# A transformer kernel on one Trainium2 core: later projections, earlier norms, idle products, signs on GpSimd and half of the stacks on ScalarE

## The chip, the core and the metric

The kernel runs on one core of a Trainium2 chip. A core has TensorE (PE in the profile; PEld is its loading of weights), VectorE (DVE), ScalarE (ACT), GpSimd (POOL) and SyncE (SP), which run side by side, each with its own queue of instructions in a fixed order; semaphores make one wait for another. SBUF is the core's working memory, PSUM the memory that TensorE writes its products to. The metric is the time of one execution on the device in microseconds (us), as a median over runs. Everything is computed in float32.

## The reference

Input x has 8 batches of 512 tokens of 256 elements. Four sublayers follow one another, each added to the residual:

```python
x = x + attn_a(layernorm(x))   # 8 heads of 64, keys and values through a rank of 64, softmax
x = x + ffn(layernorm(x))      # two layers, below
x = x + attn_b(layernorm(x))   # 16 heads of 16, below
x = x + ffn(layernorm(x))      # the same weights again

# ffn, each of two layers:
q, k, v = split(shift_token(x) @ wqkv)               # 8 heads of 64
q, k = rotary_xpos(l2norm(q) * qs, l2norm(k) * ksc)
x = x + local_attention(q, k, v) @ wo                # windows of 128, looking back one window
h = layernorm(shift_token(x)) @ w1 + b1              # to 2 x 682
a, g = split(h);  x = x + (a * gelu(g)) @ w2 + b2

# attn_b:
scores = dot * dot / (|q|^2 + |k|^2 - 2 * dot + 1e-6)   # causal
out = softmax(scores) @ v @ w_out + b_out
```

## The kernel before

The 8 batches are worked off in two groups of 4. A group passes through ten stages: attention_a, block x (attention_f and feedforward of layer 0, then of layer 1), attention_b, and block y (the same four as block x). All residuals of a group lie in SBUF; a batch is four tiles of 128 tokens (NT = 4). So the kernel has 8 attention_f stages, 8 feedforward stages and 2 attention_b stages.

A stage is a head and a `run`. While a stage runs, it calls `ahead()`, which emits a piece of the next stage's head; what is left of the head is emitted after it. Within a stage the order of each engine's instructions is written by hand: under `order_keeper` every instruction is tied to the one before it on its engine in program order.

**attention_f** (L453) works on nt = 16 tiles of 128 queries. `a_step` (L732) handles tile `step`: two units (even and odd, four heads each) of scores, maxima (L614), exponentials, `divided` (L679: the reciprocal of the sums on DVE, then four ACT operations that scale the probabilities), `turn` (L646, transposes on PE into PSUM), `keep_turned` (L657, the copy to SBUF on DVE) and `values` (L671). `keep_values` (L690) copies the tile's output, `project` (L696) multiplies it with wo, `add` (L706) adds it to `ys`, the stage's residual. Each step projects the tile of the step before. In the last steps (`projecting` false) no queries and keys of further tiles are left to be made.

**feedforward** (L805) goes through the four batches: `hidden` makes the products with w1 and gelu, `output` (L879) those with w2. `batch(n)` (L907) slips the statistics, norms and transposes of the next batches (`others`) in between.

**attention_b** (L960) works on units: one of 4 query tiles of a batch, a pair of heads (`qp`) and one to four column blocks `js`. There are 22 units a batch, 88 a group. Ahead of them stand, per batch, `normalized` (L963: `row_statistics` L256, whose inverse root is on POOL at L252 and L253, and `normalize_rows` L266) and `stacks_and_values` (L977): transposes, then 8 `side_piece`s and 2 `value_piece`s. A side piece makes one stack of heads of queries (left) or keys (right): products on PE (L1000), their squares on ACT (L1010), the squared norms added by PE (L1013), and `keep_side` (L1022 to L1028), which writes the stack st_b to SBUF with a bias and a scale, on DVE. The pieces of batch 0 are the stage's head; those of the next batches are laid one by one into the steps of the batch before (`a_piece`, L1261), and two more pieces (L1232, a turn prt and a projection pp) follow each query tile.

One unit passes through five steps: products den and dot (L1099, PE); the inverse of den by Ln and Exp (L1112, L1113, both through `function`, L227, on ACT); its error t and refinement r (L1118, L1122, DVE); squares of dot (L1128, ACT) with the causal mask (L1131, POOL); `highest` (L1134): on DVE a fused product with maximum per head (L1139) and the negation of the maxima (L1149); the exponentials (L1157 through L227, ACT), biased with the negated maxima; transposes ppt (L1169, PE), the copy pt (L1174, DVE) and the values o (L1184, PE). `each_part` (L1270) writes the order of one step by hand: the products of unit s, the dot of s-1, the maxima of s-2, the turns of s-3 and, every other step, the values of two units. The norms of batches 1, 2 and 3 are issued in steps 0 and 1, 20 and 21, 42 and 43 of the group.

In PSUM the pool `ps_s` has three buffers of two banks, for den, dot and the pieces; `ps_mm` and `ps_o` have one each, for ppt and o.

Of the kernel before, what the change touches and what calls it, by code (L numbers as in the profile page):

```python
# [11 lines left out]
F32 = mybir.dt.float32  # L12
# [5 lines left out]
P = 128  # L18
# [11 lines left out]
W1_COLS = 2 * FULL + GATES + REST  # L30
DEPTH = 2
LN_EPS = 1e-5
EPS_B = 1e-6
# [4 lines left out]
GELU_TABLES = "gelu_and_others"  # L38
Piece = namedtuple("Piece", "heavy first act second dve", defaults=(None, None, None, None))
Unit = namedtuple("Unit", "n product inverse error refine squares highest exponentials turn keep_turned values project")  # L40
ISSUE_ORDER = mybir.DependencyInfo(mybir.DependencyClass.NoSync, mybir.DependencyReason.DATA)
# [4 lines left out]
def kernel(  # L46
# [101 lines left out]
    vec_b = load(b_vec, [P, 2, 4, 2], "vec_b")  # L148
    sel_b = load(b_sel, [P, 2, P], "sel_b")

    def weights_f(l, name):
# [132 lines left out]
    def halves_of(rows):  # L284
        return [rows[:, :, 0:P], rows[:, :, P:D]]


# [165 lines left out]
    def attention_f(batches, l, g, ys, first_layer):  # L453
# [225 lines left out]
        def divided(unit):  # L679

            at, quad = divmod(unit, 2)
            p, s = ps[unit], sums[at]
            some = slice(4 * quad, 4 * quad + 4)
            nc.vector.reciprocal(s[:, some], s[:, some])
            for odd in range(2):
                for j in range(2):
                    h = 4 * quad + 2 * j + odd
                    nc.scalar.activation(p[:, odd, j], p[:, odd, j], AF.Identity, scale=s[:, h : h + 1])
# [20 lines left out]

        nt, nu = len(tiles), 2 * len(tiles)  # L710

        def on(f, at, count=nt):
# [10 lines left out]
        def rows(at):  # L723
            b, t = tiles[at]
            if first_layer and t == 0:
                normalize_rows([xs[b]], [ys[b]], *stats.pop(b))

# [4 lines left out]
        def a_step(step):  # L732

            even, odd = 2 * step, 2 * step + 1
            projecting = step + 2 < nt
            if not projecting:
                on(turn, even - 1, nu)
                on(keep_turned, even - 1, nu)
# [10 lines left out]
            if not projecting:  # L749
# [3 lines left out]
                on(maxima, odd, nu)  # L753
            on(divided, even, nu)
            on(rotate, step + 2)
            if projecting:
# [6 lines left out]
            if projecting:  # L763
                on(exponentials, odd, nu)
                on(keep_values, step - 1)
                on(turn, even, nu)
                on(keep_turned, even, nu)
                on(norms, step + 2)
                on(turn_tile, step + 1)
                on(keep_tile, step + 1)  # L770
                on(project, step - 1)
            else:
                on(project, step - 1)
                on(turn_tile, step + 1)
                on(keep_tile, step + 1)
                on(exponentials, odd, nu)
                on(turn, even, nu)
                on(keep_turned, even, nu)
            on(divided, odd, nu)
            on(values, even, nu)  # L780
            on(add, step - 1)
            on(statistics, step + 5)
# [21 lines left out]

    def feedforward(batches, l, g, ys, last, finish):  # L805
        w1, w2 = weights_g(l, g)
# [100 lines left out]
        def batch(n):  # L907

            others = [(statistics, n + 1), (rows, n + 1), (shift, n + 2)]
            others += [(lambda b, k=k: columns(b, k), n + 1) for k in range(2)]  # L910
            for _ in hidden(batches[n]):
                if others:
                    part, m = others.pop(0)
                    if m < len(batches):
                        with kept_order():
                            part(batches[m])
                yield
# [16 lines left out]
        def run(ahead):  # L934
            for n, b in enumerate(batches):
                if n:
                    for _ in batch(n):
                        if n == len(batches) - 1:
                            ahead()
                            ahead()  # L940
                output(b, made.pop(b))

        return head(), run

    def feedforward_block(batches, g, finish):

        ys = {}

        def attention(l):
            if l == 0:  # L950
                for b in batches:
                    ys[b] = resid.tile([P, NT, D], F32, tag=f"y{b % GROUP}", name=f"y_{g}_{b}")
            return attention_f(batches, l, f"{g}{l}", ys, l == 0)

        for l in range(DEPTH):
            yield lambda l=l: attention(l)
            yield lambda l=l: feedforward(batches, l, f"{g}{l}", ys, l == DEPTH - 1, finish)


    def attention_b(batches, g):  # L960
        wl_b, wr_b, wv_b, wo_b, bv_b = weights_b(g)

        def normalized(b):  # L963

            got = {}

            def statistics():
                got["mv"], got["rstd"] = row_statistics([xs[b]], f"b{b}")

            def rows():  # L970
                yr = pool.tile([P, NT, D], F32, tag="yr", name=f"yr_b{b}", bufs=1)
                normalize_rows([xs[b]], [yr], got["mv"], got["rstd"])
                state[b] = {"yr": yr}

            return [Piece(False, dve=statistics), Piece(False, dve=rows)]

        def stacks_and_values(b):  # L977
# [16 lines left out]
            def side_piece(side, w, j):  # L994
# [27 lines left out]
                def keep_side():  # L1022
# [5 lines left out]
                    )  # L1028

                return Piece(True, project, squared, norms, keep_side)  # L1030

# [33 lines left out]
        def prologue(b):  # L1065
            for piece in normalized(b):
                whole(piece)
                yield
            for piece in stacks_and_values(b):
                whole(piece)  # L1070
                yield
# [5 lines left out]

        state = {}

        def unit(b, i, qp, js, first, last):  # L1080
# [45 lines left out]
            def squares(dot):  # L1126
                num = pool.tile([P, 2, T], F32, tag="p", name=f"num_{n}", bufs=3)
                nc.scalar.activation(num[:, :, :cols], dot[:, :, :cols], AF.Square, scale=-0.5)  # L1128
                for m in range(len(js)):
                    own = per_head(num)[:, :, m, past:]  # L1130
                    nc.gpsimd.tensor_add(own, own, causal.unsqueeze(1).to_broadcast([P, 2, P]))  # L1131
                return num

            def highest(num, r):  # L1134
# [3 lines left out]
                for at, (a, m, h) in enumerate(heads):  # L1138
# [9 lines left out]
                    )  # L1148
                nc.vector.tensor_scalar_mul(most[:, 8 : 8 + nh], most[:, :nh], -1.0)  # L1149
                return most  # L1150
# [48 lines left out]
            def project(sums):  # L1199
# [9 lines left out]
                def turned():  # L1209
                    got["prt"] = ps_s.tile([P, 2, 4, P], F32, tag="s", name=f"prt_{n}")[:, 0]  # L1210
                    for k in range(4):
                        nc.tensor.transpose(got["prt"][:, k, :], rows[:, k * P : (k + 1) * P], ident)

# [19 lines left out]

            return Unit(n, product, inverse, error, refine, squares, highest, exponentials, turn, keep_turned, values, project)

# [7 lines left out]

        def run(ahead):

# [15 lines left out]
            def a_piece(s):  # L1261
# [3 lines left out]
                for some, may in ((projections, s % 2 or len(projections) % 2 == 0), (prologues, ready), (projections, True)):  # L1265
                    if some and may:
                        return some.popleft()
                return Piece(False)

            def each_part(s):  # L1270
# [6 lines left out]
                if with_values:  # L1277
                    for u in (s - 5, s - 4):
                        projections.extend(units[u].project(sums.pop(u)))
                piece = a_piece(s)  # L1280

# [26 lines left out]
                if unit_of(2):  # L1308
                    most[s - 2] = units[s - 2].highest(num[s - 2], r.pop(s - 2))
                if unit_of(3):  # L1310
                    units[s - 3].keep_turned(turned, pt[s - 3], 0)
                    turned = units[s - 3].turn(num.pop(s - 3), 1)
# [5 lines left out]
                if unit_of(3):  # L1318
                    units[s - 3].keep_turned(turned, pt[s - 3], 1)
                do(piece.dve)  # L1320
                if norms:
                    do(norms.popleft().dve)

            for step in range(count + 5):
                if step % each == 0:
# [4 lines left out]
                    if following < len(batches):  # L1330
                        if following == 1:
                            norms.extend(normalized(batches[1]))
                        prologues = deque(stacks_and_values(batches[following]))
                elif step % each == each - 2 and step // each + 2 < len(batches):
                    norms.extend(normalized(batches[step // each + 2]))
                with kept_order():
                    each_part(step)
                if step > count - 6:
                    ahead()
            with kept_order():  # L1340
                while projections:
                    whole(projections.popleft())

        return prologue(batches[0]), run

# [6 lines left out]
    for g in range(NB // GROUP):  # L1352
        batches = list(range(g * GROUP, (g + 1) * GROUP))
        stages.append(lambda batches=batches, g=g: attention_a(batches, g))
        stages.extend(feedforward_block(batches, f"{g}x", None))
        stages.append(lambda batches=batches, g=g: attention_b(batches, g))
        stages.extend(feedforward_block(batches, f"{g}y", store))
# [106 lines left out]
```

## Time and profile before

| what | value |
|---|---|
| median of 3 runs | 4530.55 us (4523.1 to 4535.95) |
| the profiled execution's own time | 4521.22 us |
| its span | 4519.4 us |
| mean granted TensorE clock | 0.965 of full speed |
| PE busy | 4197.8 us (93%) |
| DVE busy | 3138.2 us (69%) |
| ACT busy | 2695.9 us (60%) |
| POOL busy | 1183.9 us (26%) |
| attention_b, first step of a group to its drain | 1038 to 1532 us, 3288 to 3776 us |

The profile records each instruction with its engine, its line and its tiles. A group of instructions is written "line engine operation out<-in", with the number of instructions, their busy time and the mean of one, and the idle time of the engine ahead of them with what ended it. In the slices each digit is a tenth of busy time in a fortieth of the span; PEclk is the clock granted to TensorE. Names end in what they belong to: `_b` is attention_b, `_f0x` attention_f of layer 0 in block x, `_g0x` its feedforward.

### The profile page before, as it was taken

How to read it: one execution, taken by the hardware profiler on the slowest of the kernel's cores; microseconds unless marked ns; L12 is line 12 of the kernel's file. 1: busy time of each engine (PE TensorE's matmuls, PEld its weight loads, DVE VectorE, ACT ScalarE, POOL GpSimd, SP SyncE). 2: the span in 40 equal slices, each digit the busy share in tenths (PEclk: the TensorE clock that was granted, in tenths of full speed). 3: DMA queues.
4: the chain of work that ended last, by engine and by line, in shares of the span. 5: the costliest groups of instructions: out<-in, count | busy, mean ns of one | idle time of the engine just before them, and what ended most of it. 6: DMA issues, size and time to landing. Idle time of an engine off the chain costs nothing. (4 is left out here: it accounts for less than half of the span.)

```text
span 4519.4 us, 68348 instructions
## 1 busy us (share of the span) xinstructions
PE 4197.8 (93%) x25504; PEld 2569.5 (57%) x25504; DVE 3138.2 (69%) x7688; ACT 2695.9 (60%) x6316; POOL 1183.9 (26%) x1076
## 2 busy tenths in 40 slices
PE   9999999998888799999999999999988878999999
PEld 5666656554544465566556665565544544655655
DVE  6678647738999787377466786476389997864773
ACT  5767527617788676177167674275178786752761
POOL 0024224312222243143100242242122222422431
PEclk9999999999898799999999999999998888999999
DMA  2000000000000000000100000000000000000000
GB/s 81 1 22 4 23 22 3 22 5 20 1 1 1 19 3 6 4 23 13 52 29 1 20 3 23 22 3 24 3 20 1 1 1 20 3 6 22 3 4 23
DMA packets 51083, 63.22 MB, mean 14 GB/s; under 512 B 6336, under 2 KB 45504, under 8 KB 50752
## 3 DMA queue, kind: packets, MB, share of 16 engines
q1 hardware_dynamic: 50752, 58.85, 3.9%
q8 instruction: 203, 3.33, 0.3%
q14 instruction: 128, 1.05, 0.1%
HBM read 46.28 MB, written 4.19 MB: 11 GB/s over the span
## 5 line engine op out<-in xcount | busy, mean ns | idle before, releaser
L1169 PE MATMUL ppt_b<-ident,num_b 128*128 128x128 f32 x1280 | 245.9, 315 | 152.8 <-DVE pt_b L1174 136.0
L1131 POOL TENSOR_TENSOR num_b<-num_b,causal 128x256 f32<-128x256 f32 x256 | 197.1, 783 | 663.5 <-ACT num_b L1128 572.8
L1169 PEld LDWEIGHTS ppt_b<-ident,num_b 128*128 128x128 f32 x1280 | 153.3, 156 | 339.5 <-ACT num_b L227 99.9
L227 ACT ACTIVATE num_b<-num_b,most_b 128x512 f32<-128x512 f32 (+3 forms) x512 | 280.6, 554 | 23.8 <-DVE most_b L1149 20.0
L1139 DVE CUSTOM_DVE_ANT_0 num_b<-num_b,r_b 128x512 f32<-128x512 f32 (+3 forms) x512 | 249.9, 535 | 5.9 <-POOL num_b L1131 5.9
L1174 DVE COPY pt_b<-ppt_b 128x512 f32<-128x512 f32 (+1 forms) x352 | 223.6, 635 | 36.3 <-PE ppt_b L1169 34.9
L227 ACT ACTIVATE r_b<-den_b 128x1024 f32<-128x1024 f32 (+1 forms) x176 | 166.3, 945 | 136.1 <-PE den_b L1099 70.3
L1099 PE MATMUL den_b<-st_b,st_b 18*128 18x384 f32 (+3 forms) x1024 | 239.8, 523 | 7.3 <-DVE t_b L1118 5.1
L227 ACT ACTIVATE p_a<-s_a,nm_a 128x512 f32<-128x512 f32 x256 | 173.7, 684 | 109.7 <-DVE nm_a L376 105.4
L1099 PE MATMUL dot_b<-st_b,st_b 16*128 16x384 f32 (+3 forms) x1024 | 215.1, 522 | 1.4 <-ACT num_b L1128 1.4
L376 DVE TENSOR_REDUCE nm_a<-s_a 128x2 f32<-128x1024 f32 x128 | 156.5, 1223 | 69.6 <-PE s_a L372 69.6
L1118 DVE TENSOR_TENSOR t_b<-den_b,r_b 128x1024 f32<-128x1024 f32 (+1 forms) x176 | 196.8, 1118 | 9.8 <-ACT r_b L227 8.9
L227 ACT ACTIVATE p_f0y<-p_f0y,nm_f0y,rn_f0y 128x256 f32<-128x256 f32 (+1 forms) x256 | 143.8, 564 | 91.4 <-DVE nm_f0y L614 91.3
L227 ACT ACTIVATE p_f1y<-p_f1y,nm_f1y,rn_f1y 128x256 f32<-128x256 f32 (+1 forms) x256 | 143.8, 564 | 91.1 <-DVE nm_f1y L614 91.0
L1122 DVE SCALAR_TENSOR_TENSOR r_b<-t_b,r_b 128x1024 f32<-128x1024 f32 (+1 forms) x176 | 197.8, 1124 | 0.1
L227 ACT ACTIVATE p_f0x<-p_f0x,nm_f0x,rn_f0x 128x256 f32<-128x256 f32 (+1 forms) x256 | 143.7, 564 | 84.9 <-DVE nm_f0x L614 84.8
L227 ACT ACTIVATE p_f1x<-p_f1x,nm_f1x,rn_f1x 128x256 f32<-128x256 f32 (+1 forms) x256 | 143.7, 564 | 83.8 <-DVE nm_f1x L614 80.1
L390 ACT ACTIVATE p_a<-p_a,sums_a 128x512 f32<-128x512 f32 x256 | 171.8, 720 | 27.0 <-DVE sums_a L388 27.0
L227 ACT ACTIVATE r_b<-r_b 128x1024 f32<-128x1024 f32 (+1 forms) x176 | 172.5, 980 | 5.6
L517 POOL TENSOR_TENSOR ro_f1x<-ro_f1x,rs_f1x 128x512 f32<-128x512 f32 x64 | 80.3, 1277 | 361.1 <-DVE nm_f1x L614 144.1
L517 POOL TENSOR_TENSOR ro_f0x<-ro_f0x,rs_f0x 128x512 f32<-128x512 f32 x64 | 80.3, 1276 | 361.3 <-DVE nm_f0x L614 144.1
L1128 ACT ACTIVATE num_b<-dot_b 128x1024 f32<-128x1024 f32 (+1 forms) x176 | 164.8, 937 | 0.0
(345 smaller groups left out, 11249.3 us busy)
## 6 DMA issues: line engine op xcount, KB each, us to landing
x<-in_x SPq DMA_DIRECT2D x8, 512.0 KB
out<-x SPq DMA_DIRECT2D x8, 512.0 KB
wf_0x<-in_f_wqkv SPq DMA_DIRECT2D x2, 1536.0 KB
wf_0y<-in_f_wqkv SPq DMA_DIRECT2D x2, 1536.0 KB
wf_1x<-in_f_wqkv SPq DMA_DIRECT2D x2, 1536.0 KB
wf_1y<-in_f_wqkv SPq DMA_DIRECT2D x2, 1536.0 KB
wg_0x<-in_f_w SPq DMA_DIRECT2D x2, 1386.0 KB
wg_0y<-in_f_w SPq DMA_DIRECT2D x2, 1386.0 KB
```

Source lines behind the costliest of these rows:

```text
L227: i = nc.scalar.activation(out, in_, func, **more).ins
L376: nc.vector.tensor_reduce(nm, s, AX.X, ALU.max, negate=True)
L390: nc.scalar.activation(p[:, odd], p[:, odd], AF.Identity, scale=some[:, odd : odd + 1])
L517: i = nc.gpsimd.tensor_add(ro[:, c], ro[:, c], rs[:, c]).ins
L1099: return nc.tensor.matmul(s[:, a, m * width : (m + 1) * width], lhsT=left[at, j, past:width], rhs=right[at, j, :width], start=True, stop=True,
L1118: nc.vector.tensor_mul(t[:, :, :cols], den[:, :, :cols], r[:, :, :cols])
L1122: nc.vector.scalar_tensor_tensor(r[:, :, :cols], t[:, :, :cols], 2.0, r[:, :, :cols], ALU.subtract, ALU.mult)
L1128: nc.scalar.activation(num[:, :, :cols], dot[:, :, :cols], AF.Square, scale=-0.5)
L1131: nc.gpsimd.tensor_add(own, own, causal.unsqueeze(1).to_broadcast([P, 2, P]))
L1139: nc.vector.tensor_tensor_reduce(out=s4[:, a, m, :], in0=s4[:, a, m, :], in1=r4[:, a, m, :], scale=-1.0, scalar=LOWEST, op0=ALU.mult, op1= ...
L1169: nc.tensor.transpose(ppt[:, k, :], p[:, a, k * P : (k + 1) * P], ident)
L1174: nc.vector.tensor_copy(pt[:, a, :nblocks, :], ppt[:, :nblocks, :])
```

## The change

It consists of six edits.

1. attention_f: projections pass through a queue (`due`). Steps nt-4 and nt-3 no longer project; the steps after them project twice, once behind `divided(even)` and once behind `keep_turned(even)`. The last unit's division is two DVE products in place of four ACT operations.
2. The norms of batches 0, 1 and 2 of attention_b are made in the last feedforward of block x, those of batch 3 at step 6. The rows lie in the space of `y{b}`.
3. Steps 0 and 1 of attention_b (`EARLY_STEPS`) become part of its head; in that feedforward they are emitted ahead of the last `output`.
4. `kept_awake` is a product of 128x128x512 whose result nothing reads. One stands behind each turn prt (16 a group) and one in each step without a piece (26 a group).
5. The masks on POOL are issued after `highest`, and the negation of the maxima moves from DVE to POOL, ahead of them.
6. Of the 64 stacks those with odd j are written by ACT (`keep_side_late`, the last ACT operation of the step), the others by DVE as before.

```diff
+    scaled_b = const.tile([P, 2, 4], F32, name="scaled_b")
+    nc.vector.tensor_mul(scaled_b, vec_b[:, :, :, 0], vec_b[:, :, :, 1])
...
             nc.vector.reciprocal(s[:, some], s[:, some])
+            if unit == nu - 1:
...
+                for odd in range(2):
+                    nc.vector.tensor_mul(
...
+                return
...
+            on(due.append, step - 1)
+            deferring = step in (nt - 4, nt - 3)
...
             on(divided, even, nu)
+            if not projecting:
+                project_next()
+                add_projected()
...
-                on(project, step - 1)
+                if not deferring:
+                    project_next()
             else:
-                on(project, step - 1)
...
                 on(keep_turned, even, nu)
+                project_next()
...
-            on(add, step - 1)
+            add_projected()
...
+            if norms and n == 2:
+                others.append((lambda b: [part(batches[0]) for part in norms], n))
+            if norms and n == 3:
+                others = [(lambda _, m=m, part=part: part(batches[m]), n) for m in (1, 2) for part in norms]
...
+                if norms and n == len(batches) - 1:
+                    for _ in range(EARLY_STEPS):
+                        ahead()
                 output(b, made.pop(b))
...
+                def keep_side_late():
...
+                    nc.scalar.activation(
+                        state[b][name][:, j, :],
+                        got.pop("pu"),
+                        AF.Identity,
+                        bias=scaled_b[:, side, j : j + 1],
+                        scale=vec[:, 1:2],
+                    )
+
+                if j % 2:
+                    return Piece(True, project, squared, norms, None, keep_side_late)
...
+        def kept_awake(space):
+
+            nc.tensor.matmul(
+                space[:, 1].rearrange("p k c -> p (k c)"), lhsT=ident, rhs=wl_b[:, 0, :], start=True, stop=True
+            )
...
-                nc.vector.tensor_scalar_mul(most[:, 8 : 8 + nh], most[:, :nh], -1.0)
+                nc.gpsimd.tensor_scalar(most[:, 8 : 8 + nh], most[:, :nh], -1.0, 0.0, ALU.mult, ALU.add)
...
+                    kept_awake(prt)
...
-                return Piece(False)
+                return Piece(False, first=lambda: kept_awake(ps_s.tile([P, 2, 4, P], F32, tag="s", name=f"idle_b{s}")))
...
+                if unit_of(1):
+                    units[s - 1].masked(num[s - 1])
...
                 do(piece.dve)
+                do(piece.late)
...
-                elif step % each == each - 2 and step // each + 2 < len(batches):
-                    norms.extend(normalized(batches[step // each + 2]))
+                elif step == 6:
+                    norms.extend(Piece(False, dve=lambda part=part: part(batches[-1])) for part in norms_b)
...
+        def head():
+            yield from prologue(batches[0])
+            for _ in range(EARLY_STEPS):
+                next(rest)
+                yield
```

## The prediction

> **What bounds the kernel now.** I read the page's busy times and its 40 slices first, then windows by stage, then DVE's timeline of one step and the waits there. In every table the columns are PE, PEld, DVE, ACT, POOL (busy us, instructions); the windows add PEclk, DMA share and GB/s.
>
> ```profile
> PE 4197.8 (93%) x25504; PEld 2569.5 (57%) x25504; DVE 3138.2 (69%) x7688; ACT 2695.9 (60%) x6316; POOL 1183.9 (26%) x1076
> ...
> PE   9999999998888799999999999999988878999999
> ...
> DVE  6678647738999787377466786476389997864773
> ...
> PEclk9999999999898799999999999999998888999999
> ```
>
> PE is the bound nearly everywhere. In two places, slices 10 to 14 and 30 to 34, its share and clock sink while DVE's rises: attention_b. From the first step of each group to the drain:
>
> ```profile
> 1038.00:1532.00 494.00, 406.25 (x3248) 239.24 (x3246) 463.47 (x1074) 402.65 (x805) 128.88 (x158) 0.87 0.01 5
> 3288.00:3776.00 488.00, 402.10 (x3184) 235.38 (x3184) 462.96 (x1072) 399.90 (x803) 127.01 (x156) 0.88 0.01 3
> 500.00:550.00 50.00, 43.32 (x257) 27.42 (x256) 27.66 (x84) 24.70 (x63) 7.18 (x7) 0.97 0.13 41
> ```
>
> In attention_b DVE works 463.5 of 494 us (94%) and 463.0 of 488: it is the bound, and its 25 to 30 us of idle time are the only other thing to win. ACT (82%) and PE (82%, partly at half clock) stand close behind. The third line is the tail of an attention_f: PE loses 6.7 of 50 us. The kernel has eight such tails.
>
> Four windows of 3.4 us show what half clock follows:
>
> ```profile
> 1135.40:1138.80 3.40, 2.41 (x14) 1.02 (x12) 3.37 (x9) 2.38 (x6) 0.83 (x2) 0.97 0.00 0
> 1138.80:1142.20 3.40, 3.40 (x14) 2.92 (x12) 3.37 (x9) 3.26 (x4) 0.13 (x1) 0.53 0.00 0
> 1248.00:1251.40 3.40, 2.00 (x34) 1.33 (x37) 3.37 (x8) 3.37 (x5) 0.31 (x1) 1.00 0.00 0
> 1251.40:1254.80 3.40, 2.97 (x15) 0.96 (x7) 3.37 (x9) 3.21 (x7) 0.43 (x1) 1.00 0.00 0
> ```
>
> With only scores and turns in it (14 instructions, 2.41 us busy) the first was followed by one at 0.53. The third held 34 instructions, values among them, was busy less (2.00 us), and the clock stayed. A step with more products of any kind keeps its clock.
>
> **The change part by part.** The maxima's signs, one step of DVE:
>
> ```profile
> 1119.60 0.08 DVE L1139 DVE_READ_ACCUMULATOR2_ANT most_b<- 128x1 f32 x1
> 1119.72 0.17 DVE L1149 TENSOR_SCALAR most_b<-most_b 128x2 f32<-128x2 f32 x1
> 1119.80 0.55 DVE L1174 COPY pt_b<-ppt_b 128x384 f32<-128x384 f32 x1
> ```
>
> The copy starts 0.08 after the negation and the negation 0.04 after the accumulator's end, so each holds DVE between 0.08 and 0.20 us. I take 0.15: 88 units a group give 13.2 us (7 to 18). On POOL the same work is short only when free:
>
> ```profile
> L252 POOL TENSOR_SCALAR rstd_f0y<-mv_f0y x2: 194/194/194, 1286.9 to 1335.1; 128x4 f32<-128x4 f32 x2
> L252 POOL TENSOR_SCALAR rstd_b<-mv_b x3: 1072/1072/1675, 1043.7 to 1283.0; 128x4 f32<-128x4 f32 x3
> ```
>
> An operation of 4 elements took 194 ns, or 1072 to 1675 ns where DVE read two SBUF tiles (the 1675 began 0.18 us after the 1.20 us r_b<-t_b,r_b of L1122). The negation starts behind the second maximum, and what DVE runs then is the copy out of PSUM, one PSUM tile (0.55 us). So I take about 0.3 us. Behind it in POOL's queue stand the masks of the next unit; they wait for the squares anyway (the mask at 1121.04, over a microsecond after). Who waits for the sign is the exponential: in four steps it began 0.32, 0.90, 1.36 and 1.89 us after the negation's end. ACT's own work (squares, 1.01 us) covers it; I price it at nothing, and at up to 1.5 us a step if that cover is gone (below).
>
> The Trainium skill, GPSIMD Engine Reference, section 1 (Specifications), says that GpSimd shares its SBUF interfaces with VectorE and contends with DVE instructions that have two SBUF inputs. The 194 against 1675 ns agree; it speaks against this move, and is the mechanism of the rival that ends slower.
>
> The stacks: 32 a group, of which 24 are made inside the steps; half of these, 12, go to ACT as its last operation of the step.
>
> ```profile
> L1026 DVE TENSOR_SCALAR st_b<-pu_b,vec_b 128x512 f32<-128x512 f32 x24 | 19.4, 810 | 5.4 <-PE pu_b L1013 5.3
> L1010 ACT ACTIVATE sq_b<-pu_b,vec_b x64: 669/687/692, 990.4 to 3641.7; 128x512 f32<-128x512 f32 x64
> ```
>
> DVE loses 12 x 0.81 = 9.7 us; ACT gains 12 x 0.69 = 8.3 (same shape, same source), 403 to 411 of some 463. It lies in ACT's wait for the next den (0.4 to 1.2 us behind such a step), so I price it at nothing; without that cover it is the 8.3.
>
> The norms: of four batches a group, three move into the last feedforward of block x, the fourth to step 6. Inside the steps batches 1 to 3 were made, so DVE loses two, each about 1.6 (statistics) + 1.3 us (rows): 5.8. In the feedforward DVE has idle time (20.25 busy of 50 us in 600 to 650, PE 49.84), so they cost nothing there. Their POOL step held DVE and starved PE: steps with norms took 9.93, 8.70 and 9.95 us against 5.2 to 5.5; that excess, some 12 us a group, is mostly half clock and idle DVE, and I count it below.
>
> The idle products: 16 with the turns and 26 in steps with no piece, two instructions each. A pair of the same shape (128x128x512) with its norm takes 1.88 us for four instructions, so 0.94 each, 39 us a group of PE's time (406 to 445 of some 463). PE waits for DVE's pt copy 1.3 to 1.5 us in a step (136 us over 176 steps in the group of ppt_b, 0.77 on average), which covers it. What they buy is clock. DVE idles 30.5 and 25.0 us a group: I take 6 back, since starts, drains and the last piece's wait stay; bounds -5 (products late before den) and +18. The three edits before free DVE 13.2 + 9.7 + 5.8 = 28.7 us; as ACT and PE would then be as full as DVE is, I let three quarters through, 21.5 (bounds 0 and 28.7).
>
> The Trainium skill, TensorE: Matmul & The Clock Gate, section HAM oscillation, wants no PE gap over about 3.4 us. By that rule alone the idle products would be needless and the sum loses their 12 us. The trace differs: the window at 1135.4 held no gap over 1 us and still lost its clock.
>
> Two early steps: attention_b's start leaves PE idle 3.3 us (1039 to 1043) and then at half clock; the scores of steps 0 and 1 now stand before the last output's 96 products (L884, 0.38 us each, 36 us of PE), under which ACT and DVE can work them off. I take 4 us a group, that idle time and a little of the half clock (0 to 8; the Exp table load, 1.28 us, moves with them).
>
> The attention_f tails: in 505 to 545 PE waits
>
> ```profile
> PE o_f0x L671 <- DVE pt_f0x L657: 2.8, 3, 1.3
> PE ppt_f0x L646 <- ACT p_f0x L688: 2.0, 2, 1.3
> PE pp_f0x L701 <- DVE oT_f0x L693: 0.6, 1, 0.6
> ```
>
> Two projections of four products (L701, 0.379 us each, 1.5 a projection) now lie in those waits for pt, and work that stood elsewhere goes: 0.8. The last division is
>
> ```profile
> 526.94 1.28 ACT L221 ACT_TABLE_LOAD   x1
> 528.23 1.71 ACT L688 ACTIVATE p_f0x<-p_f0x,sums_f0x 128x256 f32<-128x256 f32 x4
> ```
>
> over 1.7 us on ACT behind a table load, against two DVE products of 128x512 (a like product at L548 takes 0.684): ready perhaps 1 us sooner, as DVE is not full there. Together 1.5 us a tail (0 to 3.5), eight times: 12.
>
> **Sum.** A group: 21.5 + 6 + 4 = 31.5; two: 63; with the tails 75. The profiled execution took 4521.22 us (span 4519.4), so 4446 for it. The runs' median of 4530.55 stands 9.3 above, so **4455** for the median.
>
> **Rivals.** (A) The sum: 4455, and 4430 to 4490 as its own range.
> (B) All of it converts: DVE stays the only bound, the clock holds. 2 x (28.7 + 18 + 8) + 8 x 3 = 133: 4397. For it: DVE at 1.00 in nearly every full-clock slice. Against: ACT at 411 + waits.
> (C) Three engines are full: what DVE loses becomes waits for den and for exponentials, and the idle products take PE's slack. Only starts and tails remain, 4 + 6: about 4520. For it: in group 0 ACT waits 33.4 us for dot, 38 times, so PE sets steps too:
>
> ```profile
> ACT r_b L227 <- PE dot_b L1099: 33.4, 38, 2.8
> ACT num_b L227 <- DVE most_b L1149: 5.5, 4, 3.0
> ```
>
> (D) Slower. The sign on POOL falls into a two-input DVE operation in most steps. At 1.68 against 0.17 it is 1.5 us late; less the four slacks above that is 1.18, 0.60, 0.14 and 0: mean 0.48, x 176 = 84 us; with the stacks' 24 x 0.69 = 17 no longer covered, against 12 + 8 from tails and starts: +81, the extreme. At 1.07 (0.9 late) only one slack in four is overrun, 0.58/4 x 176 = 26: about +22. Middle +50: 4580. It decides once the negation takes over about 1 us in half of the steps. For it: ACT waits only 4 times (5.5 us) for the maxima now, in the second of these lines, because DVE brings the signs itself. Against: the copy behind.
> (E) The idle products don't hold the clock but cost: 84 x 0.94 = 79 us of PE, a third uncovered, 26, and no 12: 4455 + 38 = 4493.
>
> **How the numbers follow.** A 0.46, B 0.16, E 0.08, C 0.11, D 0.19. A run differs from no change when it is more than 0.3% off (4517 to 4544). Faster: A, B, E and a fifth of C: 0.73; within: the rest of C, 0.08; slower: D, 0.19. The range reaches from B's 4395 up over C to 4545 and leaves out most of D and B's far side.
>
> **What would show it.** DVE's busy time in the 88 steps falls from 463 to about 435 a group, the stretch itself to about 465; PEclk rises from 0.87 to over 0.93, and the group of the exponentials still waits little for most_b. POOL's negation at about 0.3 us shows the move right, at over 1 us in many steps rival D. PE's wait for pt_b shrinks by the idle products if they are covered; ACT's wait for dot grows in C. The tails' PE idle falls from 6.7 to about 5. I am wrong if DVE's work falls and the step doesn't shorten.

## The result, and the profile after

| | before | after |
|---|---|---|
| median of 4 runs | 4528.1 us (4523.1 to 4535.95) | 4463.74 us (4459.31 to 4469.85) |
| span of the profiled execution | 4519.4 us | 4457.5 us |

The ratio is 0.9857, with a 95% interval of 0.9838 to 0.9876: 64 us faster, where 75 were forecast. The page of the changed kernel:

```profile
PE 4198.1 (94%) x25672; PEld 2537.4 (57%) x25672; DVE 3112.7 (70%) x7497; ACT 2697.5 (61%) x6316; POOL 1209.4 (27%) x1252
...
DVE  6678637747999787377466786477389997864773
...
PEclk9999999999999999999999999999999999999999
```

The clock's dip in slices 10 to 14 and 30 to 34 is gone. To compare like with like I cut both attention_b stages from the third step (the first that lies in the stage in both kernels) to the last. Windows of the kernel before, then of the changed one (columns as in the prediction):

```profile
1045.30:1531.90 486.60, 402.46 (x3193) 236.33 (x3192) 458.62 (x1064) 397.59 (x800) 127.30 (x157) 0.87 0.00 1
3293.10:3777.80 484.70, 399.93 (x3192) 233.90 (x3192) 460.00 (x1064) 397.49 (x799) 127.30 (x156) 0.88 0.00 1
```

```profile
1036.80:1501.20 464.40, 401.70 (x3235) 223.69 (x3234) 431.68 (x932) 402.34 (x811) 135.83 (x236) 0.96 0.02 6
3252.30:3720.10 467.80, 406.28 (x3234) 225.87 (x3234) 431.22 (x932) 402.66 (x811) 135.83 (x235) 0.95 0.02 6
500.00:550.00 50.00, 47.47 (x274) 29.30 (x271) 30.63 (x88) 23.36 (x60) 7.53 (x7) 1.00 0.13 42
```

DVE works 26.9 and 28.8 us less; the stretch is only 22.2 and 16.9 us shorter, so DVE's idle time in it grew, from 28.0 and 24.7 us to 32.7 and 36.6. The attention_f tail loses 2.5 of 50 us of PE where it lost 6.7.

From the last output product of the feedforward to that third step, before and after:

```profile
1034.90:1045.30 10.40, 6.89 (x82) 5.50 (x80) 6.19 (x14) 4.96 (x5) 3.12 (x4) 0.89 0.61 209
```

```profile
1035.30:1036.80 1.50, 1.50 (x27) 1.05 (x26) 1.40 (x4) 0.00 (x0) 0.81 (x2) 1.00 0.06 7
```

10.4 us became 1.5, in both groups; the feedforward, which now also makes norms and two steps, takes 2.7 and 4.4 us longer. Stage by stage, the difference of the two spans (61.9 us) comes from the steps (22.2 + 16.9 = 39.1), the starts (6.2 + 4.5 = 10.7) and the attention_f and feedforward stages outside (12.0 together, those behind attention_b's drain 0.7 us slower each).

The signs on POOL (least, median and longest in ns), and the last division of an attention_f on DVE's timeline. In names such as `f0x` the digit is the group (0 or 1), not the layer as said above; both layers of a block share the name. This is the first attention_f of group 0:

```profile
L1205 POOL TENSOR_SCALAR most_b<-most_b x176: 191/192/202, 1035.6 to 3743.0; 128x2 f32<-128x2 f32 x128, 128x4 f32<-128x4 f32 x32, 128x8 f32<-128x8 f32 x16
```

```profile
526.36 0.18 DVE L690 RECIPROCAL sums_f0x<-sums_f0x 128x4 f32<-128x4 f32 x1 [0.61 <-ACT p_f0x L230]
526.57 1.29 DVE L697 TENSOR_TENSOR p_f0x<-p_f0x,sums_f0x 128x512 f32<-128x512 f32 x2
```

None of the 176 negations was held up: 162 of them ran beside VectorE's copy pt_b. In the steps ScalarE waited 3.7 us a group for a sign, 5 and 6 times. The division ends 1.5 us after its reciprocal begins; before it was 3.0 (526.95 to 529.94), behind the table load.

### The profile page after: what moved, and what is told of

The parts are those of the page before. It is cut to its first block, busy times and chain, and to the rows that moved or that the text cites. A ratio compares the mean times of both kernels' runs of the same rounds, so it can differ in the third digit from the quotient of the medians.

```text
span 4457.5 us, 68762 instructions
## 1 busy us (share of the span) xinstructions
PE 4198.1 (94%) x25672; PEld 2537.4 (57%) x25672; DVE 3112.7 (70%) x7497; ACT 2697.5 (61%) x6316; POOL 1209.4 (27%) x1252
## 4 chain that ended last, share of the span: by engine, by line
PE 75%; DVE 13%; ACT 8%; POOL 2%; issue 1%; DMA 0%; SPq 0%; POOLq 0%; ACTq 0%; DVEq 0%
PE pu_g1x L891 3%; PE pu_g0x L891 3%; PE pu_g0y L891 3%; PE pu_g1y L891 3%; PE s_a L378 3%; PE o_a L414 3%; PE ppt_a L403 3%; PE pqk_f0y L481 2%; PE pqk_f1y L481 2%; PE pqk_f1x L481 2%; PE pqk_f0x L481 2%; DVE pt_b L1230 2%; DVE r_b L1176 2%; PE ppt_b L1225 2%; DVE num_b L1195 2%; PE pp_a L432 1%
## 5 line engine op out<-in xcount | busy, mean ns | idle before, releaser
L1225 PE MATMUL ppt_b<-ident,num_b 128*128 128x128 f32 x1280 | 226.5, 294 | 104.8 <-DVE pt_b L1230 84.2
L1225 PEld LDWEIGHTS ppt_b<-ident,num_b 128*128 128x128 f32 x1280 | 139.3, 144 | 289.7 <-ACT num_b L230 92.4
L1153 PE MATMUL den_b<-st_b,st_b 18*128 18x384 f32 (+3 forms) x1024 | 212.2, 476 | 4.8 <-ACT yT_b L1031 4.1
L1153 PE MATMUL dot_b<-st_b,st_b 16*128 16x384 f32 (+3 forms) x1024 | 195.7, 477 | 0.0
```

The lines of the kernel that those rows point to most:

```text
L1153: return nc.tensor.matmul(s[:, a, m * width : (m + 1) * width], lhsT=left[at, j, past:width], rhs=right[at, j, :width], start=True, stop=True,
L1225: nc.tensor.transpose(ppt[:, k, :], p[:, a, k * P : (k + 1) * P], ident)
```

## The experiments

Each kernel was run beside the kernel before; the ratio is to that one, and the changed kernel's own is 0.9857. "Span" is the profiled execution's, beside 4457.5 (changed) and 4519.4 (before). W is the theory that DVE's work set the steps, C that the clock did.

| run | median us | ratio (95% interval) | span us |
|---|---|---|---|
| e1_no_idle | 4474.88 | 0.9894 (0.9879 to 0.9909) | 4467.5 |
| e2_sign_dve | 4477.73 | 0.9904 (0.9889 to 0.9919) | 4473.3 |
| e3_stacks_dve | 4462.25 | 0.9871 (0.9855 to 0.9888) | 4460.2 |
| e4_idle_first | 4444.11 | 0.9826 (0.9809 to 0.9842) | 4446.4 |
| e5_only_idle | 4516.46 | 0.9976 (0.9967 to 0.9986) | 4515.0 |
| e6_no_early | 4490.68 | 0.9923 (0.9908 to 0.9938) | 4489.2 |
| e7_tail_act | 4475.84 | 0.9887 (0.9871 to 0.9902) | 4469.4 |
| e8_tail_only | 4511.25 | 0.9963 (0.9948 to 0.9978) | 4509.7 |
| e9_first_dve | 4439.84 | 0.9809 (0.9794 to 0.9823) | 4437.9 |
| e10_norms_back | 4485.77 | 0.9909 (0.9892 to 0.9925) | 4483.1 |
| e11_three_early | 4451.95 | 0.9838 (0.9823 to 0.9852) | 4449.6 |

How far one profile can be trusted: e3 and e5 reached the first attention_f 4 us later than the kernel that each edits, in an attention_a that neither touches. A term below some 5 us can't be read from one span. The profiled execution of the changed kernel was also the fastest of its four, that of e4 the slowest of its four, so the ratios are read beside the spans.

**Clock or work.** The changed kernel without idle products, and the kernel before with them alone:

```diff
-                return Piece(False, first=lambda: kept_awake(ps_s.tile([P, 2, 4, P], F32, tag="s", name=f"idle_b{s}")))
+                return Piece(False)
...
-                    kept_awake(prt)
```

> The changed kernel (4463.7 us) without its 84 idle products. Theory W (the work taken from VectorE shortened the steps; clock matters little): half-clock time in the 88 steps goes back to some 100 us a group, but the time rises by only 4 to 14 us, to 4468 to 4478; the stretch from the third to the last step of a group (464.4 and 467.8 us) grows by 2 to 7 us. Theory C (the clock did it): the time rises by 30 to 40 us, to 4494 to 4504.

> The kernel before (4528.1 us) with the idle products alone. Theory W: the clock is held (half clock under 50 us a group against 127 and 115), VectorE's work is unchanged, and the time falls by 0 to 12 us, to 4516 to 4528; it may even rise if the products delay den. Theory C: it falls by 30 to 40 us, to 4488 to 4498.

The steps of e1 in the same cut:

```profile
1038.00:1506.60 468.60, 397.47 (x3192) 231.84 (x3191) 434.10 (x933) 403.29 (x812) 138.74 (x236) 0.89 0.02 6
3259.60:3728.60 469.00, 396.99 (x3192) 228.74 (x3192) 433.11 (x933) 403.33 (x812) 138.79 (x235) 0.90 0.02 6
```

The clock falls back to 0.89 and 0.90, half-clock time to 99 and 96 us a group as W expected, and the stretch grows by only 4.2 and 1.2 us. Behind the last step the half clock held for another 23.9 us in each group (3.4 in the changed kernel), 20.5 of them in one piece, and from the last step to the end of that attention_f 1.3 and 1.5 us are lost. In all +10 us, as W had it, of which 1.7 lie in the two attention_a stages, which the edit doesn't touch; the ratio's rise of 0.0037 (17 us, with intervals that just don't overlap) is higher. Put into the kernel before, the same products take 8.5 and 2.1 us off the steps and save 4.4 us of span and 0.0024 of ratio (11 us), with half clock at 51 and 75 us a group, a little above what W expected. C is out: the clock is worth about a sixth of the result by the spans, a quarter by the ratios, and a third of what the trace places lies behind the steps.

**The signs** back on VectorE:

```diff
-                nc.gpsimd.tensor_scalar(most[:, 8 : 8 + nh], most[:, :nh], -1.0, 0.0, ALU.mult, ALU.add)
+                nc.vector.tensor_scalar_mul(most[:, 8 : 8 + nh], most[:, :nh], -1.0)
```

> The changed kernel with the maxima's signs back on VectorE, all else as changed. Theory W: 176 negations of about 0.15 us on VectorE, seven tenths of them felt: +15 to +26 us, 4479 to 4490; VectorE's busy time in a group's steps rises by 12 to 15 us. Theory C, or that ScalarE is now the bound: within 5 us of 4463.7.

DVE's busy time in the cut rose by 12.9 us in each group (to 444.6 and 444.1) and the span by 15.8, of it 11.2 and 2.9 in the steps. That is W's mechanism, but some 55% of the work is felt in place of seven tenths, and unevenly: in the second group most of it went into DVE's idle time (36.6 us, now 26.6). The masks stay behind `highest` in this run; what their new place is worth was not tested alone.

**The stacks** all on VectorE:

```diff
-                if j % 2:
-                    return Piece(True, project, squared, norms, None, keep_side_late)
```

> The changed kernel with all stacks written by VectorE again. Theory W: 24 stacks of 0.81 us inside the steps, seven tenths of them felt: +10 to +19 us, 4474 to 4483. Rival (ScalarE is as full as VectorE, so that moving the stacks only moved the wait): within 5 us of 4463.7, ScalarE's busy time in the steps falling by 8 us a group with no effect.

Not slower: W failed here. 12 stacks of 0.81 us came back to DVE in each group, yet its busy time rose by only 4.1 and 5.0 us, in part since its refinement r_b got shorter (by 3.6 and 2.3 us in these steps); and its idle time fell, by 2.0 and 8.9 us. The group of r_b on the pages of the changed kernel and of e3:

```profile
L1176 DVE SCALAR_TENSOR_TENSOR r_b<-t_b,r_b 128x1024 f32<-128x1024 f32 (+1 forms) x176 | 206.2, 1172 | 0.2
```

```profile
L1174 DVE SCALAR_TENSOR_TENSOR r_b<-t_b,r_b 128x1024 f32<-128x1024 f32 (+1 forms) x176 | 200.3, 1138 | 0.2
```

Before it took 1124 ns. In the changed kernel those of 128x1024 took 1.35 us on average where a POOL operation ran beside them (55) and 1.21 where none did (57).

**The idle product's place.** In the changed kernel ScalarE waits for an idle product: L1130 is `kept_awake`. ScalarE's waits in the steps (us in total, times, longest):

```profile
ACT r_b L230 <- PE den_b L1153: 16.9, 14, 6.6
ACT r_b L230 <- PE dot_b L1153: 15.4, 18, 1.9
ACT rt_b L1274 <- PE prt_b L1130: 13.6, 14, 2.3
```

```diff
+                    kept_awake(prt)
                     for k in range(4):
                         nc.tensor.transpose(prt[:, 0, k, :], rows[:, k * P : (k + 1) * P], ident)
-                    kept_awake(prt)
```

> The changed kernel with the idle product of the turn prt issued ahead of its four transposes instead of behind them. Theory F: ScalarE's copy rt waits for the idle product, since this is the last write to the tile that it reads half of (rt waits 13.6 and 17.4 us a group, 14 times each); ahead of the transposes the product falls into TensorE's wait for rb (11.5 and 11.2 us a group). The wait of rt falls below 5 us a group and the time by 6 to 20 us, to 4444 to 4458. Rival: the copy is not on the way, the wait goes and the time stays within 5 us of 4463.7.

The same line of ScalarE's waits in e4:

```profile
ACT rt_b L1274 <- PE prt_b L1269: 3.2, 7, 1.4
```

The span fell by 11.1 us, the ratio by 0.0031 (14 us), with intervals that just overlap. rt reads only the half of the tile that the transposes fill, but was released by the tile's last writer.

**Both together**, the idle product first and all stacks on VectorE:

> The changed kernel with the idle product ahead of the turns and all stacks on VectorE (the two edits of the runs before that cost nothing or gained). If moving the stacks bought nothing because the refinement r_b grew (1126 to 1169 ns, beside POOL's masks) and ScalarE came later with r_b: within 6 us of the idle-first kernel's ratio of 0.9826 (4436 to 4450 beside a kernel before of 4525), with r_b back at about 1130 ns. If theory W holds for the stacks after all, now that rt's wait is gone: +10 to +19 us, a ratio of 0.985 to 0.987.

```profile
1038.70:1492.70 454.00, 401.70 (x3234) 224.92 (x3234) 434.74 (x944) 396.43 (x799) 136.46 (x236) 0.96 0.02 6
3243.20:3701.10 457.90, 403.53 (x3234) 226.00 (x3234) 435.27 (x944) 396.70 (x800) 135.32 (x235) 0.96 0.02 6
```

DVE's waits in the first group's steps, changed kernel, e4 (idle product first, stacks still on ScalarE) and e9:

```profile
DVE pt_b L1230 <- PE ppt_b L1225: 17.5, 19, 2.4
DVE t_b L1172 <- ACT r_b L230: 8.4, 16, 2.3
```

```profile
DVE pt_b L1230 <- PE ppt_b L1225: 16.0, 18, 3.0
DVE t_b L1172 <- ACT r_b L230: 7.4, 14, 2.3
```

```profile
DVE pt_b L1228 <- PE ppt_b L1223: 8.4, 11, 1.5
DVE t_b L1170 <- ACT r_b L230: 4.0, 6, 2.3
```

DVE does 3 to 4 us more than in the changed kernel, idles 13 to 14 less, and the steps are 10 us shorter in each group. At 4440 us (ratio 0.9809) it is the fastest of all, clear of the changed kernel's interval but not of e4's: beside e4 it gains 0.0017 of ratio (8 us, where at most 6 were expected), and r_b takes 1141 ns where it took 1169. The wait for r_b fell with the stacks alone (5.1 us in e3 too), that for the turned exponentials only with both edits (18.6 in e3). By these waits the stacks on ScalarE delayed what VectorE needs from it: the next r_b, and, once rt's wait is gone, the exponentials that are turned. That this delay is why moving the stacks bought nothing fits the waits; no run separates it from the longer r_b.

**Early steps and norms.** No early steps (the first diff; e11 has 3, on top of e4), and the norms of batches 1 to 3 back in the steps (the second):

```diff
-EARLY_STEPS = 2
+EARLY_STEPS = 0
```

```diff
-            if norms and n == 3:
-                others = [(lambda _, m=m, part=part: part(batches[m]), n) for m in (1, 2) for part in norms]
...
+        def normal_pieces(k):
+            return [Piece(False, dve=lambda part=part: part(batches[k])) for part in norms_b]
...
+                        if following == 1:
+                            norms.extend(normal_pieces(1))
-                elif step == 6:
-                    norms.extend(Piece(False, dve=lambda part=part: part(batches[-1])) for part in norms_b)
+                elif step % each == each - 2 and step // each + 2 < len(batches):
+                    norms.extend(normal_pieces(step // each + 2))
```

> The changed kernel with no early steps (the norms stay ahead in the feedforward). From the last output product to the third step it took 1.5 us against 10.4 before, less the 2.6 and 4.4 us by which that feedforward ended later: a loss of about 5 us a group, +10 us, 4470 to 4478. Rival (the steps only moved their work ahead): within 4 us of 4463.7.

> The idle-first kernel (ratio 0.9826) with three early steps in place of two. Without early steps the changed kernel took 32 us longer, 16 a group, of which 8 at the start of the steps. If each early step takes a pipeline's start out of the stage, a third one gives 3 to 6 us a group: ratio 0.980 to 0.9813. If two already cover the start (from the last product to the third step it takes only 1.5 us): within 4 us, 0.982 to 0.9835.

> The changed kernel with the norms of batches 1, 2 and 3 inside the steps as before; only batch 0's stay in the feedforward, as the early steps need them. Theory W: two batches' norms of 2.9 us of VectorE in each group's steps, and the starved TensorE behind them: +5.8 to +12 us a group, +12 to +24 us, ratio 0.988 to 0.991. Rival (hidden in idle time that VectorE has by now, 32 and 36 us a group): under +5 us, a ratio of 0.985 to 0.987.

Without early steps the start takes 12.2 and 13.6 us where it took 1.5, the steps 4.5 and 3.4 us more and the next attention_f 3.0 us more in the first group, while the feedforward before gets 2.2 us shorter: +31.7 us of span (2.3 of them in the attention_a stages, which the edit doesn't touch), three times what was expected. A third early step gains nothing over e4: counted from the last output product its third step begins 7.4 and 8.1 us sooner, but the feedforward grows by 6.2 and 7.0, and the stretch behind that step by 4.6 and 1.2. With the norms back the span grows by 25.6 us: the steps they stand in grow again (step 21 to 8.4 us, 43 to 8.5 and 9.5, against a median of 5.3), and from the second early step, in which batch 1's now lie, to the third step it takes 13.4 us in place of 9.6.

**The attention_f tails.** The last division back on ScalarE, and the attention_f part alone in the kernel before:

```diff
-            if unit == nu - 1:
+            if False:
```

> The changed kernel with the last division of each attention_f back on ScalarE. If the division behind the table load was the tail's loss: +0.8 to 1.2 us in each of 8 tails, +6 to +10 us. If the queue of projections won it: within 3 us of 4463.7.

> The kernel before with the attention_f part of the change alone (queued projections and the last division). In the changed kernel the eight stages ended 1.5, 0.8, 2.3, 1.9, 0.6, 0.7, 2.2 and 2.0 us sooner, 12.0 in all: 4528.1 falls by 10 to 15 us, to 4513 to 4518, and the eight half-clock windows behind these tails vanish. Rival (the gain of the stages in block y came with attention_b's end, not from the tails): a fall of under 6 us.

PE's busy time between 500 and 550 us:

```profile
500.00:550.00 50.00, 45.84 (x270) 28.68 (x271) 28.95 (x85) 26.16 (x68) 8.63 (x8) 1.00 0.12 41
```

is e7's; 43.32 before, 47.47 with both. So the queue gave 2.5 and the division 1.6 us of PE there. By the stages, the division on ScalarE costs each attention_f 0.6 or 0.7 us, and the feedforward behind it 0.2 or 0.3: 6 to 7 in eight. Of the rest of e7's 11.8 us of span, 3.8 lie in the first group's steps and 1.3 in the attention_a stages, which the edit doesn't touch. e8's span fell by 9.7, its ratio by 0.0037 (17 us), and no half-clock window is left at the eight tails, where seven had one. Counted to their last projections its eight attention_f stages gained 17.3 us; attention_b of the second group, in which nothing changed, took 6.8 more, at half clock for 170 us in place of 133.

## Why the prediction was right

Direction and size held, but partly because terms off in both directions made up for each other.

- **DVE is the bound of attention_b; 28.7 us a group go.** 26.9 and 28.8 went. Three quarters were to come through (21.5), and the steps gained 22.2 and 16.9. That the share came out is partly luck: steps 20 to 24 and 42 to 46, where norms had stood, alone gave 10.1 and 11.9 of it, more than the norms' own work; of the signs about half came through (e2), of the stacks nothing (e3). That less work on DVE shortens the steps is shown for the signs (e2) and the norms (e10); rival C, that nothing would come through, fell with them, and B, that all of it would, with DVE's idle time, which grew.
- **The sign on POOL takes 0.3 us and nobody waits.** 192 ns, at most 202, and 3.7 us of waiting a group. Rival D named the right mechanism for a place where it doesn't act: the copy out of PSUM stands behind the maxima, beside 162 of 176 signs. Its contention turned up elsewhere, in the refinement beside POOL's masks.
- **The stacks, 9.7 us of DVE a group at no cost on ACT.** This step was wrong. The cover that I named (ACT's wait for den) was not free time: the stack stands ahead of ScalarE's next r_b, VectorE waited 8.4 us a group for that (7.4 in e4, 4.0 in e9), and the refinement of r_b grew. Alone it is worth nothing (e3), and without rt's wait it seems to cost some 8 us (e9 against e4, by span and ratio, with intervals that overlap).
- **Idle products: 6 us of DVE's idle time come back.** The price was about right, 12 us for both groups against 10 by e1's span and 17 by its ratio, but the place only in part: 5.4 us in the steps, 2.8 behind them. DVE's idle time did not fall in the changed kernel, and without the products it is about the same (32.7 and 36.6 us with them, 34.5 and 35.9 in e1). The reading of four windows, that more products keep the clock, holds only as a tendency: the changed kernel still spent 92 us of its steps at half clock, and PE's busy time tells the windows apart better than the number of instructions (last section). The wait that they brought, of rt for the product in its own tile, was not foreseen: 11 us of span lost (e4). By that, rival E held in part: a cost of the products, though through ScalarE's wait and not through TensorE's time.
- **Early steps, 4 us a group.** Mis-sized: 6.2 and 4.5 net of what the feedforward pays, but 16 by taking them out (e6). (Beside e8, which has the tails alone, that feedforward takes 5.0 and 4.7 us longer, which leaves 3.9 and 4.2 net of the norms too.) I priced PE's idle time at the start; the 10.7 and 12.1 us that the start lost in e6 fit two of 88 steps (about 5.3 us each) taken out of a stage bound by VectorE into one bound by TensorE, where they cost 2.2. A third step cost that stage 6.2 and 7.0 (e11).
- **Norms, 5.8 us a group and a share of the excess.** Mis-sized: 12.8 (25.6 in both). The excess of the steps with norms over their neighbours, 12 us by the trace of before, was the right price; I had counted it into DVE's idle time, and so to the idle products, instead.
- **Tails, 12 us.** The stages outside attention_b gave 12.0, some 7 in attention_f and 6 in the feedforwards behind, which no longer begin at half clock, less 1.4 behind attention_b. The sum's 1.5 us a tail stood for the attention_f stages alone, so that 12 came out is partly luck; e8, the tails alone, gives 10 us by its span and 17 by its ratio.

The single parts taken out add up to more (10 + 15.8 + 2.7 + 31.7 + 25.6 + 11.8 = 97.6) than the whole brought (61.9): starts and norms share steps, and the shifts of some us in untouched stages are in each. How much of the overlap is which, the runs don't tell. On the clock, the Trainium skill (TensorE: Matmul & The Clock Gate, HAM oscillation) asks for no idle gap of PE over about 3.4 us; by that alone the idle products would be needless. The trace differs: in the steps of e1 no gap was over 3.3 us, and half-clock time still more than doubled, from 92 to 195 us. It cost little in those steps, where VectorE was the bound.

## What to carry to other kernels

Price a piece of work that starves the bound engine by the lengthening of its own step, not by its busy time; moving whole steps into a neighbouring stage with another bound can be worth whole step times, as long as that stage has room for them: two steps gained here, a third was paid back in full. "Its engine waits there anyway" is cover only if nothing that the bound engine needs stands next in that engine's queue. A dummy operation that shares a tile with real data makes the data's reader wait for it: put it ahead of the real writers.

## What the runs showed of the hardware

TensorE at half clock hardly matters to a stage bound by VectorE: 58 and 45 us more of it (41 and 51 to 99 and 96 a group) lengthened the 85 steps by 4.2 and 1.2 us. But it outlasts them: in e1 it held for 23.9 us behind the last step, and from there to the end of the next attention_f 1.3 and 1.5 us were lost.

What half clock follows can be read from the steps of the kernel before, taken in windows of 3.41 us, the length of the shortest half-clock stretch there, and laid so that each such stretch fills whole windows. Of the 211 windows at full clock, those in which PE was busy less than 2 us were followed by half clock 19 times in 25, those with 2 to 2.5 us 14 times in 44, and those with more once in 142. The number of instructions tells less: 0 to 34 in the windows that were followed by half clock, 5 to 70 in the others.
